# Two levels of Strassen for three quarters of a gated feed-forward network, with the weights' sums kept in DRAM

## The chip, the cores and the metric

The kernel runs on one core of a Trainium2 chip. The metric is the time of one execution on the device in microseconds. All data are float32.

## The reference

x has 32 rows of 64 tokens with 1024 features. Four layers are added to it, one after the other; ids choose the weights of each row:

```python
x = x + conv(x) * mask                       # a kernel K of 1024 steps, by FFT
x = x + einsum('bsi,boi->bso', x, w1[ids1])  # an adapter of 1024 x 1024 for each row
x = x + einsum('bij,bkj->bik', x, w2[ids2])  # another
gate = lora(x @ W_gate.T, A_gate, B_gate)    # W_gate, W_up: 2752 x 1024
up   = lora(x @ W_up.T, A_up, B_up)          # lora: a term of rank 16, by row
act  = silu(gate) * up
x = x + lora(act @ W_down.T, A_down, B_down) # W_down: 1024 x 2752
```

## The kernel before

Features lie on the partitions and tokens along the free axis. x is cut into four chunks of 512 tokens (eight rows). The convolution runs first, for all chunks. Then come the two adapters of the eight rows of chunk 0, and then, chunk by chunk, the feed-forward part `ffn`. While `ffn` works on a chunk, the 16 adapters of the next are slipped in between its pieces: `between` (L549) is called after every gate or up matrix of a tile and `other` (L543) after most pieces of W_down, and `other` emits an adapter when the shares handed to it say that one is due. In the first five calls `between` instead brings in the next chunk's x and adds the convolution to it (`bring`, `take`).

The 2752 hidden features are two halves of ten tiles of 128, and 192 that are left over (`rest`, L479). `gated` (L423) makes two tiles, m and m + 10, at a time, first gate, then up, each as a 2 x 2 block product in Strassen's form (Winograd's variant): `stationary` (L404) makes four sums of the four weight quarters on VectorE, and seven products replace eight. A product is four matmuls of 128 x 128 by 256 columns (L438), and each matmul is two instructions in the trace[...]. The order of the seven products, of the copies out of PSUM and of the adds is written out: 0, 5, 6, 4, 1, 2, 3. Product 4 overwrites the bank of product 5 and so needs that bank's reading done:

```python
            product(pa, 0, True)
            nc.scalar.copy(u, pa)
            product(pb, 5, True)
            nc.scalar.copy(cq[:, 3], pb)
            nc.vector.tensor_add(u, cq[:, 3], u)
            product(pc, 6, True)
            nc.vector.tensor_add(cq[:, 3], pc, u)
            product(pb, 4, True)
```

The rank-16 term of a tile is spread out by `expand` (L374) into four banks and copied by ScalarE into the tile `lt`, of which there is one; the add at L467 ends its use. After both matrices ScalarE takes the sigmoid, and VectorE multiplies twice.

W_down runs in two blocks of five m (`BLOCKS`), each after its gated tiles, by one level of Strassen as well (L630). Its moving sums come from act (`actd`, L587), its weights' sums from `stationary`, in segments of three m; the results are added into x. The rank term's columns of A_down are loaded by `columns` (L313), through the tile raw and eight DMAs of GpSimd's queue, and low_rank_down (L363) uses them after the first segment. `prepare` (L516) makes the four moving sums of x for the next chunk and copies three of its quarters on ScalarE (`xd`).

TensorE's order is the order of the program. The order of the other engines is set by a scheduler within what the dependences allow; within an engine instructions then start in that order. Weights come through `wpool`, nine buffers of 4 KB per partition in rotation, loaded by SP's queue. PSUM is eight banks in rotation (`ps_tile`). The pools apool, gpool and hpool hold what lives longer; a tile with `bufs=1` waits for the last use of the tile before it with the same tag.

Of the kernel before, what the change touches and what calls it, by code (L numbers as in the profile page):

```python
# [16 lines left out]
P = 128  # L17
# [10 lines left out]
BLOCKS = ((0, FM // 2), (FM // 2, FM))  # L28
MB = FM // 2
# [4 lines left out]
SEG = 3  # L34
TH = TC // 2
KH = KT // 2
R = 16
# [3 lines left out]
STEPS = 5  # L41
AT_GATED, AT_DOWN = 4, 5
# [27 lines left out]
def kernel(  # L70
# [18 lines left out]
    bd: bass.AP,  # L89
    wr: bass.AP,  # L90
# [212 lines left out]
    def b_rows(c, piece):  # L303
# [5 lines left out]
        tc.tile_pool(name="apool", bufs=MB, side="right", reuse_waits="tile")  # L309
    )  # L310
    cols = []

    def columns(table, c, n, name):  # L313

        raw = gpool.tile([P, BC, n, R], F32, tag="raw", name=f"raw_{name}", bufs=1)
# [47 lines left out]
    def low_rank_down(at, acts, name, last):  # L363
        v = gpool.tile([P, 2 * H], F32, tag="tv", name=f"tv_{name}", bufs=2)
        ps = low_rank(at, len(acts), lambda i: acts[i], name)
        nc.vector.tensor_mul(v, ps, bmask)
        if last is not None:
            nc.vector.tensor_add(v, v, last)
            for j in range(BC // 2):
                t = rest2[pair(j % 2), j // 2, 2 * H * (j % 2) :][:, : 2 * H]  # L370
                nc.vector.tensor_copy(t, v[pair(j)])
        return v
# [31 lines left out]
    def stationary(w, n, name):  # L404


        s = gpool.tile([P, 3, KH, P], F32, tag="s", name=f"s_{name}")
        a11, a12, a21, a22 = (w[i][:, k, :n, :] for i in (0, 1) for k in (0, 1))
        s1, s2, s4 = (s[:, i, :n, :] for i in range(3))
        nc.vector.tensor_add(s1, a21, a22)  # L410
        nc.vector.tensor_sub(s2, s1, a11)
        nc.vector.tensor_sub(a21, a11, a21)
        nc.vector.tensor_sub(s4, a12, s2)
        return a11, a12, s4, a22, s1, s2, a21
# [8 lines left out]
    def gated(c, m, xb, between):  # L423

        lt = expand(b_rows(c, m), f"{c}_{m}", (("g", 0), ("g", 1), ("u", 2), ("u", 3)))
        lt = lt.rearrange("p (g i) t -> p g i t", g=2)
        cs = []
        for g, w in enumerate((wg, wu)):
            name = f"{c}_{m}_{g}"
            wt = []  # L430
            for i in (0, 1):
                t = wpool.tile([P, 2, KH, P], F32, tag="w", name=f"wf{i}_{name}")
                nc.sync.dma_start(t.rearrange("p k s f -> p (k s f)"), w[i, m])
                wt.append(t)
            ws = stationary(wt, KH, name)
# [12 lines left out]
            pa, pb, pc = (ps_tile(f"pf{i}_{name}")[:, :TH] for i in range(3))  # L448
            cq = gpool.tile([P, 4, TH], F32, tag=f"c{g}", name=f"c_{name}", bufs=1)
            u = gpool.tile([P, TH], F32, tag="u", name=f"u_{name}")  # L450
# [3 lines left out]
            nc.scalar.copy(cq[:, 3], pb)  # L454
            nc.vector.tensor_add(u, cq[:, 3], u)
            product(pc, 6, True)
            nc.vector.tensor_add(cq[:, 3], pc, u)
            product(pb, 4, True)
            nc.vector.tensor_add(cq[:, 3], pb, cq[:, 3])  # L459
            product(pa, 1, False)  # L460
            nc.scalar.copy(cq[:, 0], pa)
            product(pb, 2, False)
            nc.vector.tensor_add(cq[:, 1], pb, u)  # L463
            product(pc, 3, False)
            nc.vector.tensor_add(cq[:, 2], pc, u)  # L465
            cf = cq.rearrange("p q t -> p (q t)")
            done = nc.vector.tensor_add(cf, cf, lt[:, g].rearrange("p i t -> p (i t)"))  # L467
            last_add.append(done.ins)
            cs.append(cq)
            between(2 * m + g)  # L470

        act = apool.tile([P, 2, TC], F32, tag="act", name=f"act_{c}_{m}")
        a = act.rearrange("p i (t n) -> p (i t) n", t=2)
        nc.scalar.activation(a, cs[0], AF.Sigmoid)
        nc.vector.tensor_mul(a, a, cs[0])
        nc.vector.tensor_mul(a, a, cs[1])
        return act

    def rest(c):  # L479


        bt = b_rows(c, FM)
        for i in range(3):
# [9 lines left out]
            elif i == 0:  # L493
                pss = []
                cr = gpool.tile([P, 3, KH, P], F32, tag="s", name=f"cr_{c}")
# [19 lines left out]

    def prepare(c, name):  # L516

        x_c = xs[c]
        at = columns(ag if name == "g" else au, c, KT, f"{name}_{c}")
# [10 lines left out]
        xd = hpool.tile([P, 7, KH, TH], F32, tag="xd", name=f"xd_{c}")  # L530
        for i, q in enumerate((0, 2, 3)):
            nc.scalar.copy(xd[:, 4 + i], xq[q])
        xb = moving(*xq, *(xd[:, i] for i in range(4)))
        return (xd[:, 4], xd[:, 5], xd[:, 6], *xb[3:])

    def ffn(c, xb, others):
# [6 lines left out]
        def other(share, of=(2 * FM - STEPS) * AT_GATED + (2 * KH - 3) * AT_DOWN):  # L543
# [4 lines left out]

        def between(i):  # L549

            if i < STEPS:
                if c + 1 < NCK:
                    if i in (2, 4):
                        take(c + 1, (i - 2, i - 1))
                    if i in (0, 2):
                        bring(c + 1, (i, i + 1))
            else:
                other(AT_GATED)

        rest(c)  # L560
        tv = None
        for block, (m0, m1) in enumerate(BLOCKS):
            last = m1 == FM
            n = 2 * MB + (0 if last else 2)
            at = columns(ad[:, block, :, :n], c, n, f"d{block}_{c}")
            acts = []
            for m in range(m0, m1):
                acts.append(gated(c, m, xb, between))
            ins = [act[:, i, :] for i in (0, 1) for act in acts]
            if last:  # L570


                wl = gpool.tile([P, 2, 2, L // 2], F32, tag="wl", name=f"wl_{c}", bufs=1)
# [6 lines left out]
            else:  # L580
# [3 lines left out]
            for i, act in enumerate(acts):  # L584
                t3 = apool.tile([P, 4, TH], F32, tag="actd", name=f"actd_{c}_{m0 + i}")
                q = [act[:, h, t * TH : (t + 1) * TH] for h in (0, 1) for t in (0, 1)]
                ab.append(moving(*q, *(t3[:, j] for j in range(4))))  # L587

            for h in range(KH):
# [9 lines left out]
                for s0 in range(m0, m1, SEG):  # L599
                    nt = min(SEG, m1 - s0)  # L600
                    end = s0 + nt == m1

                    more = int(end and not last)
                    at_ = s0 + block
# [12 lines left out]
                    elif end:  # L617
                        w = [[wl[:, t, i, h * P : (h + 1) * P] for i in (0, 1)] for t in (0, 1)]
                        tails = {1: (w[0][0], 0), 3: (w[0][1], 0), 4: (w[1][1], 1), 2: (w[1][0], 1)}
                    ws = stationary(wt, nt, f"{name}_{s0}")  # L620
                    for j in (0, 5, 6, 4, 1, 3, 2):
                        if end and j in tails:
                            w, t = tails[j]
                            a = rest2[:, t] if last else rest1[:, t * TH : (t + 1) * TH]
                            nc.tensor.matmul(  # L625
                                pss[j], w, a, start=False, stop=False, skip_group_check=True
                            )
                        for i in range(nt):
                            m = s0 + i
                            nc.tensor.matmul(  # L630
                                pss[j],
                                ws[j][:, i, :],
                                ab[m - m0][j],
                                start=(m == m0 and home[j] % 2 == 0),
                                stop=(m == m1 - 1),
                                skip_group_check=True,
                            )
                    if h == 0 and s0 == m0:
                        tv = low_rank_down(at, ins, f"d{block}_{c}", tv if last else None)
                u = gpool.tile([P, 3, TH], F32, tag="uo", name=f"uo_{name}", bufs=1)  # L640
# [21 lines left out]
                if not last or h < KH - 3:  # L662
# [319 lines left out]
def _layouts(np, v):  # L982
# [43 lines left out]


# [4 lines left out]
    wd = np.concatenate([wd[..., :MB, :], left1, wd[..., MB:, :]], axis=4)  # L1032
# [9 lines left out]
    a = a.reshape(2, 2, MB, P, NE, R).transpose(4, 1, 3, 0, 2, 5)  # L1042
# [71 lines left out]
```

## Time and profile before

| | us |
|---|---|
| median of three runs | 2381.4 (2378.52 to 2382.32) |
| the profiled execution: its own time | 2377.0 |
| its span | 2375.4 |
| convolution and first loads (0 to 191.9) | 191.9, TensorE busy 156.7, DMA share 0.93 |
| adapters of chunk 0 (191.9 to 343.88) | 152.0, TensorE busy 130.3, DMA share 1.01 |
| feed-forward part of chunk 2 | 536.9, TensorE busy 536.0, DMA share 0.62 |

The other three feed-forward parts are shown with the prediction. VectorE is busy for 256 us of the 537 us of a chunk, ScalarE for 66, GpSimd for 31. The matmuls in the records overlap (a row gives 381 ns for one whose successor starts 216 ns later), so a busy time is read as covered time and not as a sum of durations. Of the 505.41 MB that DMA moves, 15 MB are written to DRAM.

### The profile page before, as it was taken

How to read it: one execution, taken by the hardware profiler on the slowest of the kernel's cores; microseconds unless marked ns; L12 is line 12 of the kernel's file. 1: busy time of each engine (PE TensorE's matmuls, PEld its weight loads, DVE VectorE, ACT ScalarE, POOL GpSimd, SP SyncE). 2: the span in 40 equal slices, each digit the busy share in tenths (PEclk: the TensorE clock that was granted, in tenths of full speed). 3: DMA queues.
4: the chain of work that ended last, by engine and by line, in shares of the span. 5: the costliest groups of instructions: out<-in, count | busy, mean ns of one | idle time of the engine just before them, and what ended most of it. 6: DMA issues, size and time to landing. Idle time of an engine off the chain costs nothing.

```text
span 2375.4 us, 46146 instructions
## 1 busy us (share of the span) xinstructions
PE 2311.7 (97%) x19154; PEld 1839.0 (77%) x19154; DVE 1098.0 (46%) x2078; ACT 309.6 (13%) x605; POOL 190.3 (8%) x275
## 2 busy tenths in 40 slices
PE   5999889999999999999999999999999999999999
PEld 5986437777777787777777787777777787888888
DVE  7411116543355535543345535553445535554653
ACT  4200002100011102110011102110011102110210
POOL 4322001000000010000000010000000010000000
PEclk9999999999999999999999999999999999999999
DMA  8999994666766654666766654566766653223311
GB/s 300 368 342 361 407 391 125 217 229 218 268 228 246 210 164 139 206 239 218 278 219 243 219 169 132 202 245 222 271 222 233 223 163 112 80 78 109 96 56 63
DMA packets 165987, 505.41 MB, mean 213 GB/s; under 512 B 20354, under 2 KB 54402, under 8 KB 165266
## 3 DMA queue, kind: packets, MB, share of 16 engines
q1 hardware_dynamic: 147874, 463.87, 55.5%
q0 software_dynamic: 11104, 29.93, 3.7%
q10 hardware_dynamic: 6800, 8.65, 1.0%
q8 instruction: 151, 2.47, 0.4%
q14 instruction: 58, 0.48, 0.1%
HBM read 487.41 MB, written 14.97 MB: 211 GB/s over the span
## 4 chain that ended last, share of the span: by engine, by line
PE 90%; DMA 7%; DVE 2%; issue 1%; ACT 0%; SPq 0%; POOL 0%; DVEq 0%; ACTq 0%
PE pf L438 40%; PE po L630 21%; PE pa L269 16%; PE pc L915 4%; DMA wa<-in_w 4%; PE pr L499 4%; PE po L625 2%; PE pe L382 2%; DMA hk<-kp 1%; PE pl_d L354 1%; DVE x L232 0%; DMA wf<-in_wg 0%; DVE br L717 0%; PE pl_u L354 0%; PE pl_g L354 0%
## 5 line engine op out<-in xcount | busy, mean ns | idle before, releaser
L438 PE MATMUL pf<-xd,wf 128*128 128x256 f32 x2560 | 606.4, 381 | 0.0
L438 PEld LDWEIGHTS pf<-xd,wf 128*128 128x128 f32 x2560 | 481.9, 190 | 74.3 <-issue 6.2
L269 PE MATMUL pa<-wa,x 128*32 128x256 f32 x7872 | 453.4, 380 | 19.2 <-DMA wa<-in_w 17.1
L438 PE MATMUL pf<-xd,s 128*128 128x256 f32 x1920 | 454.1, 379 | 2.7 <-DVE c L459 2.2
L269 PEld LDWEIGHTS pa<-wa,x 128*32 128x32 f32 x7872 | 245.4, 110 | 216.0 <-DMA wa<-in_w 46.3
L438 PEld LDWEIGHTS pf<-xd,s 128*128 128x128 f32 x1920 | 364.3, 190 | 54.2 <-DVE c L459 3.7
L915 PE MATMUL pc<-uf,hk 128*128 128x256 f32 (+7 forms) x1024 | 151.7, 309 | 11.3 <-DMA hk<-kp 6.5
L630 PE MATMUL po<-act,wd 128*128 128x256 f32 x640 | 161.7, 383 | 0.0
L630 PE MATMUL po<-actd,s 128*128 128x256 f32 x640 | 159.0, 379 | 0.0
L630 PE MATMUL po<-actd,wd 128*128 128x256 f32 x640 | 159.0, 379 | 0.0
L915 PEld LDWEIGHTS pc<-uf,hk 128*128 128x128 f32 x1024 | 146.7, 193 | 15.6 <-issue 7.9
L296 POOL DMA_INDIRECT bgu<-in_bgu,rows x44 | 46.4, 1054 | 1328.7 <-PE pe L382 1257.8
L463 DVE TENSOR_TENSOR c<-pf,u 128x256 f32<-128x256 f32 x80 | 34.0, 425 | 235.3 <-PE pf L438 235.3
L630 PEld LDWEIGHTS po<-act,wd 128*128 128x128 f32 x640 | 119.5, 190 | 22.9 <-issue 6.3
L630 PEld LDWEIGHTS po<-actd,s 128*128 128x128 f32 x640 | 121.6, 190 | 16.5
L630 PEld LDWEIGHTS po<-actd,wd 128*128 128x128 f32 x640 | 121.6, 190 | 16.5
L392 ACT COPY lt<-pe 128x512 f32<-128x512 f32 x160 | 82.1, 599 | 335.8 <-PE pe L382 249.8
L279 DVE STREAM_TRANSPOSE y<-pa 128x512 f32<-128x512 f32 x64 | 45.6, 712 | 118.9 <-PE pa L269 118.9
L467 DVE TENSOR_TENSOR c<-c,lt 128x1024 f32<-128x1024 f32 x80 | 98.0, 1224 | 5.5 <-DVE c L465 0.5
L410 DVE TENSOR_TENSOR s<-wf 128x512 f32<-128x512 f32 x80 | 54.9, 686 | 87.9 <-DMA wf<-in_wg 45.5
L410 DVE TENSOR_TENSOR s<-wd 128x384 f32<-128x384 f32 x64 | 31.2, 488 | 133.8 <-PE po L630 87.4
L499 PE MATMUL pr<-x,wr 128*128 128x512 f32 x192 | 84.2, 595 | 0.0
(169 smaller groups left out, 1830.8 us busy)
## 6 DMA issues: line engine op xcount, KB each, us to landing
wa<-in_w SPq DMA_DIRECT2D x492, 512.0 KB, 7.5
wf<-in_wg SPq DMA_DIRECT2D x80, 512.0 KB, 3.9
wf<-in_wu SPq DMA_DIRECT2D x80, 512.0 KB, 3.7
wd<-in_wd SPq DMA_DIRECT2D x96, 384.0 KB, 4.6
hk<-kp SPq DMA_DIRECT2D x30, 1024.0 KB, 8.4
x<-in_xt SPq DMA_DIRECT2D x4, 2048.0 KB, 11.1
uf<-in_xf SPq DMA_DIRECT2D x16, 512.0 KB, 5.3
early<-in_w SPq DMA_DIRECT2D x16, 512.0 KB, 6.3
```

The source lines that it names most:

```text
L269: nc.tensor.matmul(acc[i * S : (i + 1) * S, s * 256 : (s + 1) * 256], xs[c][:, kt, lo + s * S : lo + (s + 1) * S], wt[:, i * 256 : (i + 1) ...
L279: nc.vector.transpose(y, acc)
L296: nc.gpsimd.indirect_dma_start(out=t, out_offset=None, in_=table, in_offset=bass.IndirectOffsetOnAxis(ap=at_, axis=0),)
L382: nc.tensor.matmul(ps[:, at_ * 2 * H : (at_ + 1) * 2 * H], bt[pair(j), g], tms[table][pair(j)], start=(g == 0), stop=True, skip_group_chec ...
L392: nc.scalar.copy(lt[:, :n, 2 * H * j : 2 * H * (j + 1)], ps[:, : n * 2 * H].rearrange("p (i t) -> p i t", i=n),)
L410: nc.vector.tensor_add(s1, a21, a22)
L438: nc.tensor.matmul(ps, ws[j][:, kt, :], xb[j][:, kt, :], start=start and kt == 0, stop=kt == KH - 1, skip_group_check=True,)
L467: done = nc.vector.tensor_add(cf, cf, lt[:, g].rearrange("p i t -> p (i t)"))
L499: nc.tensor.matmul(ps, wt[:, kt, :], xs[c][:, kt, :], start=(kt == 0), stop=(kt == KT - 1),)
L625: nc.tensor.matmul(pss[j], w, a, start=False, stop=False, skip_group_check=True)
L630: nc.tensor.matmul(pss[j], ws[j][:, i, :], ab[m - m0][j], start=(m == m0 and home[j] % 2 == 0), stop=(m == m1 - 1), skip_group_check=True,)
L915: nc.tensor.matmul(ps[:, j, d * B :], hk[:, j, d * P : (d + 1) * P], uf[:, i + j, : KT - d, :].rearrange("p k b -> p (k b)"), start=(d == ...
```

## The change

W_gate and W_up of chunks 1 to 3 are multiplied by two levels of Strassen. `gated` now handles two m at once (a group gi, five in a chunk): it runs one pass for gate and one for up, in chunk 0 by `halves`, afterwards by `quarters`.

- `halves` keeps the matmuls of before for the two m. Beside them VectorE makes the second level's sums of the weights (`kept`, four times in a pass), and GpSimd's queue writes these and the first level's sums (`kept_parts`) to tiles in DRAM (`sums`, `parts`).
- `quarters` runs seven outer products (the second index of `xb`), each made of seven inner ones of two matmuls with 128 columns. The outer products go in units: three pairs, (0, 5), (1, 6) and (4, 2), and a single one, (3,). A pair shares its PSUM banks and its tile `t`, of which there is one. Weights and their sums are loaded from a new input `wq`, `parts` and `sums`, two tiles (`wb`, `wa`) to an outer product. Three banks serve a pair, four the single unit.
- The sigmoid, the multiply by it and the second multiply are done in two halves of 1024 columns.
- `prepare` makes 7 x 7 tiles of moving sums for chunks 1 to 3.
- W_down has three blocks, of two, four and four m. A_down's columns are requested after a block's gated tiles and share the tag of `t`, as does the tile `uo` of W_down's evictions; `wl` has the tag of `lt`, and the columns of A_gate and A_up that of the sigmoid's tile.
- The shares by which adapters are slipped in are new, and `between` is called after the second pair and at the end of a pass.

```diff
-BLOCKS = ((0, FM // 2), (FM // 2, FM))
-MB = FM // 2
+BLOCKS = ((0, 2), (2, 6), (6, FM))
+MB = 4
+MG = 2
+NG = FM // MG
...
-SEG = 3
+SEG = (2, 4, 2)
...
-AT_GATED, AT_DOWN = 4, 5
+AT_GATED, AT_DOWN = 3, 5
...
+        raw = gpool.tile([P, BC, n, R], F32, tag=tag, name=f"raw_{name}", bufs=1)
...
+    def sides(a11, a12, a21, a22, s1, s2, s3, s4):
+        nc.vector.tensor_add(s1, a21, a22)
+        nc.vector.tensor_sub(s2, s1, a11)
+        nc.vector.tensor_sub(s3, a11, a21)
+        nc.vector.tensor_sub(s4, a12, s2)
+        return a11, a12, s4, a22, s1, s2, s3
...
+    def low_rank_of(c, gi, g):
+        name = f"{c}_{gi}_{g}"
+        lt = expand(b_rows(c, 2 * gi + g), name, [("gu"[g], i) for i in range(4)])
+        return lt.rearrange("p (i m) t -> p i m t", i=2)
...
+    def halves(c, gi, g, o, xb, between):
+        name = f"{c}_{gi}_{g}"
+        w = (wg, wu)[g]
+        lt = low_rank_of(c, gi, g)
+        wts, sts, sides_of = [], [], []
...
+            st = s_tile((gpool, qpool[0])[m], f"{name}_{m}")
+            wts.append(wt)
+            sts.append(st)
+            sides_of.append(stationary(wt, KH, st))
...
+        def kept(q):
+            src = [
+                [wts[m][0] for m in range(MG)],
+                [wts[m][1] for m in range(MG)],
+                [sts[m][:, 0:2] for m in range(MG)],
+                [sts[m][:, 2:3] for m in range(MG)],
+            ][q]
+            n = 1 if q == 3 else 2
+            t = qpool[0].tile([P, 2, 4, KQ, P], F32, tag="kept", name=f"kept{q}_{name}", bufs=2)
+            a11, a12, a21, a22 = (
+                src[m][:, :, k * KQ : (k + 1) * KQ, :] for m in range(MG) for k in range(2)
+            )
+            sides(a11, a12, a21, a22, *(t[:, :n, i] for i in range(4)))
+            nc.gpsimd.dma_start(
+                sums[2 * gi + g][2 * q : 2 * q + n].rearrange("j p e -> p j e"),
+                t[:, :n].rearrange("p j i k f -> p j (i k f)"),
+            )
...
+            if m == 0:
+                kept_parts()
+            kept(2 * m)
...
+            kept(2 * m + 1)
+            o_m = o[:, :, m]
+            done = nc.vector.tensor_add(o_m, o_m, lt[:, :, m])
+            between()
+        last_add.append(done.ins)
...
+    def quarters(c, gi, g, o, xb, between):
+        name = f"{c}_{gi}_{g}"
+        lt = low_rank_of(c, gi, g)
+        at_sums = {0: 0, 1: 1, 6: 2, 3: 3, 4: 4, 5: 5, 2: 6}
+        at_parts = {6: 0, 4: 1, 5: 2, 2: 3}
+        raw = {0: 0, 1: 1, 3: 2}
+        def load(j):
+            tb = wpool.tile([P, 3, KQ, P], F32, tag="w", name=f"wb{j}_{name}")
+            src = wq[2 * gi + g, raw[j]] if j in raw else parts[2 * gi + g][at_parts[j]]
+            nc.sync.dma_start(tb.rearrange("p i k f -> p (i k f)"), src)
+            ta = wpool.tile([P, 4, KQ, P], F32, tag="w", name=f"wa{j}_{name}")
+            nc.sync.dma_start(
+                ta.rearrange("p i k f -> p (i k f)"), sums[2 * gi + g][at_sums[j]]
+            )
...
+        def unit(js):
+            n = len(js)
+            ws = [load(j) for j in js]
+            def product(ps, i, start):
+                for w, j, to in zip(ws, js, range(n)):
+                    for k in range(KQ):
+                        nc.tensor.matmul(
+                            ps[:, to * TQ : (to + 1) * TQ],
+                            w[i][:, k, :],
+                            xb[:, j, SLOT[i], k, :],
+                            start=start and k == 0 and to == 0,
+                            stop=k == KQ - 1,
+                            skip_group_check=True,
+                        )
+            js_ = "".join(map(str, js))
+            banks = [ps_tile(f"pq{i}_{name}_{js_}")[:, : n * TQ] for i in range(5 - n)]
+            pa, pb, pc, pd = (banks + banks[1:2])[:4]
+            t = gpool.tile([P, 4, 2 * TQ], F32, tag="t", name=f"t_{name}_{js_}", bufs=1)
+            c11, c12, c21, c22 = (t[:, i, : n * TQ] for i in range(4))
+            u = gpool.tile([P, 2 * TQ], F32, tag="u", name=f"u_{name}_{js_}")[:, : n * TQ]
+            product(pa, 0, True)
+            nc.scalar.copy(u, pa)
+            product(pb, 5, True)
+            nc.scalar.copy(c22, pb)
+            nc.vector.tensor_add(u, c22, u)
+            product(pc, 6, True)
+            nc.vector.tensor_add(c22, pc, u)
+            product(pd, 4, True)
+            nc.vector.tensor_add(c22, pd, c22)
+            product(pa, 1, False)
+            nc.scalar.copy(c11, pa)
+            for i in (3, 2) if n == 1 else (2, 3):
+                ps, to = ((pd, c12), (pc, c21))[i - 2]
+                product(ps, i, False)
+                nc.vector.tensor_add(to, ps, u)
...
+        add = nc.vector.tensor_add
+        c11, c12, c21, c22 = quarter(o)
+        l11, l12, _, _ = quarter(lt)
+        p1, p6 = unit((0, 5))
+        add(c12, p1, p6)
+        add(c11, p1, l11)
+        p2, p7 = unit((1, 6))
+        add(c21, c12, p7)
+        add(c11, c11, p2)
+        between()
+        p5, p3 = unit((4, 2))
+        add(c22, c21, p5)
+        add(c12, c12, p5)
+        add(c12, c12, p3)
+        (p4,) = unit((3,))
+        add(c12, c12, l12)
+        add(c21, c21, p4)
+        done = add(o[:, 1], o[:, 1], lt[:, 1])
+        last_add.append(done.ins)
+        between()
+    def gated(c, gi, xb, between):
+        f = quarters if c else halves
+        act = apool.tile([P, 2, MG, TC], F32, tag="act", name=f"act_{c}_{gi}")
+        f(c, gi, 0, act, xb, lambda: between(2 * gi))
+        sg = gpool.tile([P, 2, MG, TC], F32, tag="cu", name=f"sg_{c}_{gi}", bufs=1)
+        for i in (0, 1):
+            nc.scalar.activation(sg[:, i], act[:, i], AF.Sigmoid)
+            nc.vector.tensor_mul(act[:, i], act[:, i], sg[:, i])
+        up = gpool.tile([P, 2, MG, TC], F32, tag="cu", name=f"up_{c}_{gi}", bufs=1)
+        f(c, gi, 1, up, xb, lambda: between(2 * gi + 1))
+        for i in (0, 1):
+            nc.vector.tensor_mul(act[:, i], act[:, i], up[:, i])
         return act
...
+        for i in (0, 1):
+            b11, b12, b21, b22 = (q_of(k, t)[i] for k in (0, 1) for t in (0, 1))
+            moving(b11, b12, b21, b22, *(at_(j)[i] for j in (4, 5, 6, 3)))
+            for j, q in zip(range(3), (b11, b21, b22)):
+                nc.scalar.copy(at_(j)[i], q)
+        b11, b12, b21, b22, t1, t2, t4 = (xd[:, :, i] for i in range(7))
+        moving(b11, b12, b21, b22, t1, t2, b12, t4)
...
-        def other(share, of=(2 * FM - STEPS) * AT_GATED + (2 * KH - 3) * AT_DOWN):
+        def other(share, of=4 * (NG - 1) * AT_GATED + (KH + 1) * AT_DOWN):
...
+            if i >= 2:
                 other(AT_GATED)
+            elif c + 1 < NCK:
+                came_at[0] += 1
+                if came_at[0] == 1:
+                    bring(c + 1, (0, 1))
+                if came_at[0] == 3:
+                    take(c + 1, (0, 1))
+                    bring(c + 1, (2, 3))
...
-            at = columns(ad[:, block, :, :n], c, n, f"d{block}_{c}")
+            n = 2 * (m1 - m0) + (0 if block else 2)
             acts = []
-            for m in range(m0, m1):
-                acts.append(gated(c, m, xb, between))
-            ins = [act[:, i, :] for i in (0, 1) for act in acts]
+            for gi in range(m0 // MG, m1 // MG):
+                acts.append(gated(c, gi, xb, between))
+            at = columns(ad[:, block, :, :n], c, n, f"d{block}_{c}", "t")
...
-                wl = gpool.tile([P, 2, 2, L // 2], F32, tag="wl", name=f"wl_{c}", bufs=1)
+                wl = gpool.tile([P, 2, 2, L // 2], F32, tag="lt", name=f"wl_{c}", bufs=1)
...
-                u = gpool.tile([P, 3, TH], F32, tag="uo", name=f"uo_{name}", bufs=1)
+                        tv = low_rank_down(at, ins, f"d{block}_{c}", tv, last)
+                u = gpool.tile([P, 3, TH], F32, tag="t", name=f"uo_{name}", bufs=1)
...
+                if block == 0 and h == 1 and c + 1 < NCK:
+                    take(c + 1, (2, 3))
+                if block == 1 or (last and h < KH - 3):
...
```

## The prediction

> **What bounds the kernel now.** First the page's busy shares and the row of the granted clock, then the windows by chunk, then the chain of waits, then the matmul groups split by shape, last the timeline of one gated layer.
>
> ```profile
> PE 2311.7 (97%) x19154; PEld 1839.0 (77%) x19154; DVE 1098.0 (46%) x2078; ACT 309.6 (13%) x605; POOL 190.3 (8%) x275
> ...
> PEclk9999999999999999999999999999999999999999
> ```
>
> TensorE is busy throughout at full clock. The windows cut the span at the starts of the four chunks' feed-forward parts (columns: TensorE, its weight loads, VectorE, ScalarE, GpSimd, clock, DMA share, GB/s):
>
> ```profile
> 343.88:881.17 537.29, 536.14 (x4497) 422.30 (x4498) 255.61 (x474) 68.84 (x134) 36.87 (x58) 1.00 0.61 214
> 881.17:1417.61 536.44, 535.83 (x4498) 422.12 (x4497) 256.02 (x474) 66.10 (x132) 31.11 (x46) 1.00 0.62 214
> 1954.48:2375.40 420.92, 416.79 (x2320) 354.55 (x2319) 218.94 (x433) 58.57 (x126) 11.59 (x11) 1.00 0.28 86
> ```
>
> A chunk with adapters to slip in takes 537 us, the last 421, with no gap on TensorE. The chain of waits prices its pieces:
>
> ```profile
> 274.88 10.11 DMA wa<-in_w
> ...
> 443.49 7.04 PE pa L269 x128
> ...
> 2027.33 1.10 PE pe L382 x32
> 2028.43 24.37 PE pf L438 x112
> 2052.80 1.10 PE pe L382 x32
> ```
>
> Each row of reduced tiles (m) costs 24.37 + 1.10 = 25.47 us, back to back; an adapter 7.04 us. Before the feed-forward part an adapter's eight 512 KB loads take 10.2 us from start to start (274.88 to 285.10): 4.19 MB / 10.2 = 410 GB/s is what DMA can give.
>
> ```profile
> L438 PE MATMUL pf<-xd,wf 128*128 128x256 f32 x2560 | 606.4, 381 | 0.0
> ...
> L915 PE MATMUL pc<-uf,hk 128*128 128x160 f32 x128 | 28.1, 302 | 0.0
> ...
> L915 PE MATMUL pc<-uf,hk 128*128 128x128 f32 x128 | 24.8, 276 | 0.0
> L915 PE MATMUL pc<-uf,hk 128*128 128x96 f32 x128 | 23.3, 264 | 0.0
> ```
>
> The new matmuls have 128 columns, a form the convolution has. Its matmuls come in pairs of equal shape whose busy times overlap: a pair covers the step plus one duration, so the step is 24.8/64 us - 276 ns = 111 ns for 128 columns, 137 for 160, 100 for 96[...]. A 256-column one takes 24.37 us / 112 = 217.6 ns. Half the columns cost half the time, just.
>
> ```profile
> 2027.91 0.42 DVE L465 TENSOR_TENSOR c<-pf,u 128x256 f32<-128x256 f32 x1
> 2028.84 1.23 DVE L467 TENSOR_TENSOR c<-c,lt 128x1024 f32<-128x1024 f32 x1
> 2030.10 1.22 DVE L476 TENSOR_TENSOR act<-act,c 128x1024 f32<-128x1024 f32 x1
> 2030.16 2.05 ACT L392 COPY lt<-pe 128x512 f32<-128x512 f32 x4 [5.87 <-DVE c L467]
> 2032.04 0.42 DVE L418 TENSOR_TENSOR actd<-act,actd 128x256 f32<-128x256 f32 x1
> 2032.07 0.42 ACT L452 COPY u<-pf 128x256 f32<-128x256 f32 x1
> 2032.34 0.43 ACT L454 COPY c<-pf 128x256 f32<-128x256 f32 x1
> 2032.49 0.43 DVE L420 TENSOR_TENSOR actd<-act,actd 128x256 f32<-128x256 f32 x1
> 2033.65 1.89 PE L438 MATMUL pf<-xd,s 128*128 128x256 f32 x8
> ```
>
> This is the start of an m. The four copies of the low-rank term wait for the last add of the m before; the copies out of PSUM queue behind them and end at 2032.77; the fourth product, which overwrites that bank, starts at 2033.65. So the cover is 0.9 us, with products of 1.73 us (8 x 216 ns).
>
> [...] In the timeline the next add starts 0.34 us after a 256 one, 0.45 if it needs its result; for 512: 0.61 and 0.72, for 1024: about 1.15 and 1.26. [...]
>
> **The change part by part.** A pass is gate or up for two m's: ten in a chunk.
>
> Matmuls. A pass was 2 x 112/2 matmuls, 24.37 us; in chunks 1 to 3 it is 7 x 7 x 2 matmuls of two instructions: 196 x 0.111 = 21.76. Saved 2.6 us, x30 = **-78 us**. W_down, tails, rank terms, adapters keep their matmuls.
>
> The single unit. The seven outer products run as three pairs and a single one. A pair's product lasts 8 x 0.111 = 0.89 us, the single one's 0.44. Let E be the end of the third pair on TensorE. VectorE then owes, in the changed program's order, before the single unit's first add: c21 (starts E+0.2), three 512 adds out of t at 0.65, 1.26, 1.87 and the add of l12 at 2.59; the single's adds start at 3.2, 3.5, 3.8. Its sixth product accumulates onto the bank that the second of these reads: due at 5 x 0.44 = 2.2, it starts at 3.9. **1.7 us** lost, all 30 times; in the up passes a 1024 multiply stands in between: **2.85**. TensorE has nothing else in its order there.
>
> Into the next pass. After gate: a sigmoid multiply (1.15) sits between the single's adds, so the last add on act ends at 8.1; ScalarE does the second sigmoid (1.06, to 9.2), only then four low-rank copies (2.05), then the two PSUM copies, to 11.9. The next pass's fourth product is due at 3.1 + 1.1 + 2.7 = 6.9. It starts at 12.0: 5.1 us lost, the 1.7 included. After up, with lt free at 8.4: 2.85 + 1.5 + 0.4 = 4.75. If an adapter (7.04) lies between, it hides all but 2.1 and 3.2.
>
> Into W_down. Blocks 0 and 1 now start on the m's just made. Product two needs half 1 of act and its moving sums (start about 12 instead of 6.8): 8.3 lost before block 0; before block 1 7.3, or 3.0 with an adapter. raw for A_down shares t's slot and is requested after the block's passes: slot free at 7.8, eight GpSimd issues 7.4 us (1383.06 to 1390.43 in the trace), landing 2.8, copy 1.1: 19. Before block 2 TensorE wants it at 12.0: 2.85 + 7 = 9.9.
>
> Sums. Chunk 3 has no adapters: five 5.1, two 4.75, 8.3, 7.3, 9.9 = 60.5. In chunks 1 and 2 the shares of other() put an adapter at five of the eight pass ends of groups 1 to 4: 5.1 + 8.3 + 2.1 + 3.2 + 5.1 + 3.0 + 5.1 + 3.2 + 2.1 + 9.9 = 47. Together **+155 us** (bounds 95 and 180: the adds may close up[...]).
>
> Chunk 0. The same matmuls. VectorE gets, per pass, three times four 512 adds and four 256 ones: 3 x 4 x 0.65 + 4 x 0.37 = 9.3 us on 13.6 (4 x 0.65 x 2 sums of weights, 6.0 evictions, 2.4 multiplies), beside 25.5 of TensorE: fits on average, but the sums of the next pass's weights stand behind the last pass's multiplies, and 12 us of sums ahead of its first evictions. I work out 7.6 us for a pass without an adapter ahead and 2 with one; the first group is ordered better, and W_down's stages hide some. Four of the first and four of the second: 38; **+40** (10 to 90, as waits for kept buffers can't be seen here). Writes of 5.2 MB a pass, 52 MB in all, go beside the loads.
>
> DMA in chunks 1 and 2. A pass loads 7 x (393 + 524 KB) = 6.4 MB, and 1.3 adapters 5.5 MB: 11.9 MB in 21.8 + 1.1 + 9.3 = 32 us, 370 GB/s of 410. Nine buffers, four in use by a pair, hold one pair ahead; after an adapter in mid-pass the next pair's tiles come some 2 us late, five times a chunk: **+20** for both (0 to 80).
>
> Rest. The next chunk's xd sums, 14 us of VectorE instead of 5, spread over W_down's 14 us steps; a third block's evictions, with uo and t in one slot, delay the next pass by about 1 us: **+8** (0 to 20).
>
> Sum: -78 + 155 + 40 + 20 + 8 = +145. On the profiled execution's 2377.0 us: 2522; its time lies 4 us under the median of the runs, so **2525 us** is forecast.
>
> **The rivals.**
> - Faster (0.10). TensorE runs ahead: eight banks hold two pairs, and the adds that I put in the way are off its path. Then 78 us stay, less 20 in chunk 0: 2320. For it: VectorE is 46% busy. Against: the single unit's last two products reuse banks of the same unit. It decides if a pass loses under 2.6 us on average and chunk 0 nothing; I have 5.
> - DMA bound (0.12). If 3 KB rows and mixed writes give 300 GB/s, the eight passes with adapters last 95.4 MB / 300 = 318 us a chunk, not 260: +115 less the hidden +20: 2620.
> - Chunk 0 bound by VectorE and by kept buffers waiting for their writes (0.15): +100 in place of 40: 2585.
> - The waits are half as long (0.08): -78 + 78 + 50 = 2425.
> - No change (0.02): losses equal the gain.
>
> **How the numbers follow.** My own case has 0.53; the bounds of its terms, not all at one end at once, give 2405 to 2630, which also takes in the second, third and fourth rivals and leaves out the first. A difference under 0.2% can't be told from none here. Faster 0.10, same 0.02, slower 0.88.
>
> **What would show it.** 128-column steps of 111 ns in pq[...]. Per pass without adapters a gap on TensorE near 1.7 us in the single unit, ended by VectorE, and one near 3.4 us at the fourth product of the next pass, ended by ScalarE. Last part: about 455 us instead of 421. Chunk 0: 575 or more. Waits of pq for wa or wb above 40 us would be the DMA rival. I am wrong if TensorE stays gapless, or if the last chunk gets shorter.

## The result, and the profile after

The changed kernel takes 2628.2 us (median of four runs, 2623.9 to 2643.5), the one before 2380.7 on the same chip: a ratio of 1.105, with a 95% interval of 1.100 to 1.110. The forecast was 2525, slower by 6.0%, with a range up to 2630. The direction holds, the loss is 1.7 times the forecast one, and the measured time lies at the very end of the range, by the ratio (1.105 x 2380.7 = 2631) just beyond it. The profiled execution took 2624.3 us, with a span of 2622.6.

The page of the changed kernel, its busy shares and the row of the granted clock:

```profile
PE 2349.9 (90%) x21674; PEld 1918.9 (73%) x21674; DVE 1356.9 (52%) x2746; ACT 369.9 (14%) x814; POOL 267.2 (10%) x387
...
PEclk9999999999999998999999999999999999999999
```

TensorE's share fell from 97% to 90%. The row of tenths hides what the mean clock says: 0.967, against 1.0 before. The windows, cut at the starts of the chunks' feed-forward parts (columns as in the prediction; the clock is the third number from the end):

```profile
342.90:946.35 603.45, 561.20 (x4500) 431.81 (x4497) 359.53 (x687) 68.53 (x141) 91.51 (x126) 0.97 0.76 275
946.35:1549.12 602.77, 541.92 (x5337) 446.80 (x5336) 309.47 (x628) 85.81 (x200) 35.53 (x54) 0.96 0.74 262
1549.12:2146.00 596.88, 536.36 (x5338) 439.50 (x5337) 308.98 (x628) 85.54 (x200) 34.76 (x54) 0.97 0.74 265
2146.00:2622.60 476.60, 423.67 (x3161) 382.66 (x3159) 266.96 (x579) 80.07 (x192) 24.72 (x36) 0.94 0.51 171
```

The four parts are 66, 66, 60 and 56 us longer than before. TensorE is idle for 42 to 61 us in each (length less busy time), where it was 1 to 4. And it is busier than before, though chunks 1 to 3 have 26 us less of matmul work each. The clock tells much of why: a value of 0.94 over 476.6 us means some 57 us at half clock in the last part. In the clock's record there are 37 such stretches, each at 0.5, nearly all of 3.4 or 6.8 us, 171 us in all; TensorE was busy in 149 of them, and half of that is 74 us.

The waits of TensorE in the last part, where there are no adapters (columns: who waits, for what, us in total, times, longest):

```profile
PE pq L574 <- DVE t L595: 26.5, 10, 5.1
PE pq L574 <- ACT t L592: 10.5, 6, 2.6
PE po L835 <- DVE actd L438: 5.7, 3, 3.0
PE pl_d L368 <- ACT at_d L345: 4.7, 1, 4.7
PE pq L574 <- DVE t L597: 1.6, 1, 1.6
```

The first row is the single unit's sixth product behind VectorE, the second the next pass's fourth product behind ScalarE, then the entries into W_down and A_down's columns. These are the waits that the prediction named; only the last row, 1.6 us, is another. The timeline from a gate pass to the next up pass shows both, and what follows a wait:

```profile
2288.47 0.69 DVE L628 TENSOR_TENSOR act<-act,t 128x512 f32<-128x512 f32 x1
2289.08 0.68 DVE L629 TENSOR_TENSOR act<-act,t 128x512 f32<-128x512 f32 x1
2289.80 0.69 DVE L630 TENSOR_TENSOR act<-act,t 128x512 f32<-128x512 f32 x1
2290.52 0.69 DVE L632 TENSOR_TENSOR act<-act,lt 128x512 f32<-128x512 f32 x1
...
2291.52 0.29 DVE L595 TENSOR_TENSOR t<-pq,u 128x128 f32<-128x128 f32 x1
2291.87 0.71 PE L574 MATMUL pq<-xd,wb 128*128 128x128 f32 x4 [1.73 <-DVE t L595]
...
2292.96 1.89 PE L397 MATMUL pe<-tm_u,bgu 32*128 32x128 f32 x32
...
2294.77 2.04 PE L574 MATMUL pq<-xd,wb 128*128 128x128 f32 x8
2296.64 1.95 PE L574 MATMUL pq<-xd,wa 128*128 128x128 f32 x16
2296.94 2.02 ACT L407 COPY lt<-pe 128x512 f32<-128x512 f32 x4
...
2299.10 0.42 ACT L592 COPY t<-pq 128x256 f32<-128x256 f32 x1
...
2299.57 1.16 PE L574 MATMUL pq<-xd,wa 128*128 128x128 f32 x8 [0.98 <-ACT t L592]
```

Four adds of the old units stand ahead of the single unit's (L595), and TensorE waits 1.73 us. Then its work runs at half speed (granted clock 0.50 in the window 2293.23:2296.64): the rank matmuls take 1.89 us (1.10 in the kernel before) and the product of eight 2.04, where the 16 matmuls of the next row take 1.95. The wait behind ScalarE is then only 0.98 us; where the clock had stayed up ahead of it, it was 2.57. So slow matmuls partly fill the next wait, and their cost can't simply be added to it.

### The profile page after: what moved, and what is told of

The parts are those of the page before. It is cut to its first block, busy times and chain, and to the rows that moved or that the text cites. A ratio compares the mean times of both kernels' runs of the same rounds, so it can differ in the third digit from the quotient of the medians.

```text
span 2622.6 us, 53347 instructions
## 1 busy us (share of the span) xinstructions
PE 2349.9 (90%) x21674; PEld 1918.9 (73%) x21674; DVE 1356.9 (52%) x2746; ACT 369.9 (14%) x814; POOL 267.2 (10%) x387
## 4 chain that ended last, share of the span: by engine, by line
issue 55%; PE 18%; DMA 4%; DVE 4%; POOL 2%; POOLq 1%; ACT 0%; DVEq 0%; ACTq 0%
PE po L835 9%; PE pf L506 5%; PE pa L273 2%; POOL bgu L300 1%; DMA wa<-in_w 1%; POOLq L334 1%; DMA wf<-in_wu 1%; DMA wd<-in_wd 1%; DMA wf<-in_wg 1%; DMA raw_d<-in_ad 1%; POOL raw_d L340 1%; DMA sums<-kept 0%; PE pl_d L368 0%; DVE s L421 0%; DVE s L423 0%
## 5 line engine op out<-in xcount | busy, mean ns | idle before, releaser
L574 PE MATMUL pq<-xd,wa 128*128 128x128 f32 x3360 | 437.6, 281 | 35.7 <-ACT t L592 25.9
L574 PEld LDWEIGHTS pq<-xd,wa 128*128 128x128 f32 x3360 | 409.4, 196 | 43.2 <-ACT t L592 29.4
L574 PE MATMUL pq<-xd,wb 128*128 128x128 f32 x2520 | 350.0, 285 | 96.9 <-DVE t L595 75.1
L574 PEld LDWEIGHTS pq<-xd,wb 128*128 128x128 f32 x2520 | 315.5, 197 | 114.7 <-DVE t L595 80.8
L603 DVE TENSOR_TENSOR t<-pq,u 128x256 f32<-128x256 f32 x240 | 92.4, 390 | 169.1 <-PE pq L574 168.9
L506 PE MATMUL pf<-xd,wf 128*128 128x256 f32 x640 | 159.1, 394 | 0.0
L506 PE MATMUL pf<-xd,s 128*128 128x256 f32 x480 | 124.1, 405 | 29.2 <-DVE act L529 17.5
L506 PEld LDWEIGHTS pf<-xd,wf 128*128 128x128 f32 x640 | 126.2, 199 | 22.7 <-issue 2.9
L506 PEld LDWEIGHTS pf<-xd,s 128*128 128x128 f32 x480 | 94.7, 200 | 48.9 <-DVE act L529 20.3
L593 DVE TENSOR_TENSOR u<-t,u 128x256 f32<-128x256 f32 x120 | 46.8, 390 | 126.0 <-ACT t L592 126.0
```

The source lines that it names most:

```text
L506: nc.tensor.matmul(ps, ws[j][:, kt, :], xb[j][:, kt, :], start=start and kt == 0, stop=kt == KH - 1, skip_group_check=True,)
L574: nc.tensor.matmul(ps[:, to * TQ : (to + 1) * TQ], w[i][:, k, :], xb[:, j, SLOT[i], k, :], start=start and k == 0 and to == 0, stop=k == K ...
L593: nc.vector.tensor_add(u, c22, u)
L603: nc.vector.tensor_add(to, ps, u)
```

## The experiments

All kernels are read part by part (chunk by chunk) beside the changed kernel and each other. E1 to e9 have one execution each. Parts with the same work differ between executions: chunk 0 took 596.8 to 605.4 us in four with the changed kernel's code there, chunk 2 596.9 to 604.7, the last part 471.3 to 476.6. Smaller differences decide nothing. E1, e2, e4, e5, e7 and e8 ask which part of the change costs what; e3, e6 and the last pair ask about the clock; e9 and e10 try to mend it.

**Without the kept sums.** `kept` and `kept_parts` aren't called, and the loads of `quarters` are

```diff
-            src = wq[2 * gi + g, raw[j]] if j in raw else parts[2 * gi + g][at_parts[j]]
+            src = wq[2 * gi + g, j % 3]
...
-                ta.rearrange("p i k f -> p (i k f)"), sums[2 * gi + g][at_sums[j]]
+                ta.rearrange("p i k f -> p (i k f)"), (wg, wu)[g][j % 2, MG * gi]
```

> Chunk 0 doesn't make or write the second level's sums; chunks 1 to 3 load tiles of the same sizes from the input tensors instead, so their weights are not the right ones. My theory (the kept sums hold VectorE, which waits for their writes, and TensorE waits for VectorE): chunk 0's part goes from 603 to 540-548 us, the other parts stay within 5 us, 2565 us in all (2555 to 2578). Rival (the grouping of two m, the third block and the shared tiles cost it): chunk 0 stays above 590.

2582.4 us. Chunk 0 took 562.8: 41 us less than with the sums, but 26 more than before, so neither my theory nor the rival was right alone.

**One level everywhere.** `gated` always takes `halves`, without kept sums.

> All chunks run the one-level passes of chunk 0, without kept sums: what remains of the change is grouping, three blocks of W_down, shared tiles. My theory (the second level's waits and the half clock after them make the loss): parts of 540 to 548 us and 425 to 430 for the last, 2405 us in all (2390 to 2425), hardly any half-clock time. Rival (grouping and blocks): above 2480.

2478.4 us; the windows of chunks 1 and 3:

```profile
914.00:1475.10 561.10, 542.87 (x4498) 423.30 (x4497) 268.25 (x521) 67.06 (x137) 36.40 (x54) 0.99 0.60 204
...
2034.50:2476.70 442.20, 424.68 (x2321) 356.38 (x2319) 231.99 (x479) 61.30 (x132) 25.07 (x35) 0.99 0.29 86
```

My expectation here forgot what the prediction itself had priced, the entries into W_down: TensorE waits 9.1 us at W_down's matmuls in chunk 3. The parts are 21 to 27 us longer than before, 95 us in all, without any second level. From this kernel to the changed one the kept sums add 39 us in chunk 0, and the second level 42, 38 and 34 us in chunks 1 to 3, where it should have saved 26 each.

**Matmuls in the waits.** `fill` issues n matmuls into a PSUM bank that nobody reads:

```diff
+            if c == 3 and js == (0, 5) and (g, gi) != (0, 0) and not (g == 0 and gi in (1, 3)):
+                fill(c, name + "a", 5 if g else 2)
             product(pd, 4, True)
...
+            if n == 1:
+                fill(c, name + "b", 5 if g else 3)
             for i in (3, 2) if n == 1 else (2, 3):
```

> The changed kernel with 256-column matmuls that nobody reads put where TensorE waits: in every single unit before its sixth product (3 of them after gate, 5 after up), and in chunk 3 before the fourth product of a pass's first pair too. They take 0.435 us each, less than the wait. My theory (the waits set the clock to half for 3.4 us or more each): although TensorE has 30 us more to do in chunk 3, its part goes from 477 to 455-465 us, its half-clock time from 56 us to under 25, its idle time from 53 to 15-25; chunks 1 and 2 get 5 to 12 us shorter each; 2590 us in all. Rival (the half clock comes from the 128-column form and its many weight loads): half-clock time stays above 45 us in chunk 3, no part gets shorter, 2620 to 2640.

2619.2 us. Half-clock time fell from 171 us to 102, in chunk 3 from 56 to 15, and chunk 3 took 467.8 us with 30 us more work (471.3 to 476.6 in four executions without it). So the half clock depends on the waits, with the form of the matmuls unchanged; but the gain was smaller than I expected. The pair at the end puts a number on it.

**Adds written later, low-rank copies behind the PSUM copies.** `t` and the tiles that share its tag have two buffers, and `middle` emits the adds of the unit before (for the first pair: `low_rank_of`):

```diff
             nc.vector.tensor_add(c22, pd, c22)
+            middle()
             product(pa, 1, False)
```

> t and its tag have two buffers; the adds of a unit's results are written behind the fourth product of the next unit; the low-rank term is spread out after the fourth product of the first pair, so its four copies stand behind the two PSUM copies on ScalarE. My theory (the queue order on VectorE and ScalarE makes the waits): the single unit's wait falls from 1.73 and 2.67 us to about 1 (some old adds still stand between), the wait at the next pass's fourth product to under 1; chunk 3 from 477 to 435-448, chunks 1 and 2 from 600 to 565-580, 2530 us in all (2500 to 2560). Rival (TensorE waits for loads or for VectorE's total work): no part gets more than 10 us shorter.

2560.4 us. In chunk 3 the waits for VectorE within a pass fell from 28.1 us to 9.4, and those for ScalarE were gone:

```profile
PE pq L572 <- DVE t L593: 8.8, 10, 2.4
PE pl_d L368 <- ACT at_d L345: 5.8, 1, 5.8
PE po L846 <- DVE actd L438: 4.1, 3, 2.5
PE po L846 <- DVE act L661: 1.9, 1, 1.9
```

Chunk 3 took 435.3 us, 41 less, as expected: the order on the two queues made these waits. It is now below the 442.2 of e2, the one-level kernel with the same three blocks, but above the 421.0 of the kernel before: only beside the first does the second level pay there. Chunks 1 and 2 took 588 and 592, only 15 and 5 less: 16 us of waits for `wb` and `wa` stay in chunk 1, and the entry waits too.

**Sums made, but not written.** As e1, with the sums of `kept` kept and both writes taken out.

> Chunk 0 makes the kept sums but doesn't write them or the parts to DRAM; chunks 1 to 3 load tiles of the same sizes from the input tensors, so their weights are not the right ones. Chunk 0's part was 603 us with sums and writes and 563 with neither. My theory (VectorE stands still at a kept tile whose write hasn't landed): 566 to 578. Rival (the sums themselves are too much for VectorE): 590 or more.

2610.0 us, chunk 0 at 585.7: above my range and below the rival's. The sums on VectorE cost 23 us (585.7 - 562.8), their writes 18 (603.5 - 585.7), a figure not far above the spread of that part. Without the writes TensorE's waits for VectorE in the gated products hardly change (24.0 us with, 21.9 without); its waits for adapters' loads, 5.0 us, are gone, and the half clock is 24 us instead of 41.

**Waits of set length in the kernel before.**

```diff
             product(pb, 5, True)
+            if g == 1:
+                for _ in range((0, 8, 10, 13)[c]):
+                    nc.scalar.copy(cq[:, 3], u)
             nc.scalar.copy(cq[:, 3], pb)
```

> The kernel before with extra copies on ScalarE ahead of the copy that the fourth product of each up matrix waits for: none in chunk 0, 8, 10 and 13 in chunks 1, 2 and 3, for ten waits a chunk of about 1.0, 1.9 and 3.2 us. My theory (a wait of about 2 us or more is followed by 3.4 us at half clock): chunk 0 stays at 537; chunk 1 gets 10-14 us longer, with few half-clock windows; chunk 2 22-32 with some 5 windows; chunk 3 45-55, of which 32 are idle and the rest ten windows. Rival (a wait costs its own length): 10, 19 and 32 us and no half clock.

2491.3 us; chunks 1 to 3, and the matmuls behind one wait of 3.9 us:

```profile
885.85:1439.49 553.64, 539.85 (x4497) 422.55 (x4496) 256.65 (x474) 98.34 (x212) 31.40 (x46) 1.00 0.61 207
1439.49:2006.68 567.19, 544.75 (x4498) 426.09 (x4496) 256.55 (x474) 106.35 (x232) 31.58 (x46) 0.99 0.59 202
2006.68:2489.50 482.82, 439.78 (x2321) 368.00 (x2319) 219.97 (x433) 109.94 (x256) 11.58 (x11) 0.95 0.26 76
```

```profile
2051.21 2.51 PE L438 MATMUL pf<-xd,s 128*128 128x256 f32 x8 [3.90 <-ACT c L457]
2053.51 3.11 PE L438 MATMUL pf<-xd,wf 128*128 128x256 f32 x8
2056.46 1.89 PE L438 MATMUL pf<-xd,s 128*128 128x256 f32 x8
```

Products of 1.89 us take 2.51 and 3.11 after the wait. Chunk 3 got 61.9 us longer (421.0 before) for 39.0 us of idle time: each wait of 3.9 us cost 6.2. Sorted by length: of five waits of 0.9 us none was followed by half clock, of ten between 1.7 and 1.9 one, of five between 2.6 and 2.8 four, of ten of 3.9 all. Here a wait cost more than its length once half clock followed it, and the longer waits were followed by it more often; where they fell is counted in the last section.

**Two blocks of W_down in the one-level kernel**: blocks (0, 4) and (4, 10), in segments of 2 and 3. Some adapters of the next chunk run ahead of the second half of its convolution's adds here; their number and size is the same.

> The one-level kernel (e2) with two blocks of W_down, of four and six m, in place of three. My theory (each entry into a W_down block that starts on the m just made costs 5 us or more of waiting, and half clock after it): the parts go from 561 to 552-557, the last from 442 to 434-438, 2450 us in all. Rival (the passes of two m cost it, through ScalarE's copies of the low-rank term): parts within 3 us of the one-level kernel's.

2428.0 us. The parts took 550.6, 553.7, 553.3 and 426.2, so 6 to 16 us less. In chunk 3 the 9.1 us of waits at W_down's matmuls are gone, and the 10 us of half clock too; with whatever else the third block and the other segments cost, that is three quarters of the one-level kernel's loss there. In chunks 1 and 2 waits for adapters' weights grew (5.9 us in chunk 1).

**Everything deferred.** As e4, with the single unit's adds first and the gating written into the next pass; the third pair's adds are put behind with

```diff
+        with tc.issue_after(adds[-1]):
+            add(c22, c21, p5)
+            add(c12, c12, p5)
+            add(c12, c12, p3)
+            add(c12, c12, l12)
```

> As the later adds (e4), and: the third pair's adds and the low-rank add stand behind the single unit's own adds on VectorE; the sigmoid and the multiplies of a pass are written into the next pass, behind its fourth product; A_down's columns are requested after a block's first gate pass, through the tile of actd. My theory: in chunk 3 the single unit's wait falls below 0.5 us, no wait for ScalarE is left, the wait for A_down's columns is gone: 435 to 412-424. Chunks 1 and 2 keep their waits for DMA (16 to 20 us): 590 to 565-580. Chunk 0 595-605. 2510 us in all (2485 to 2535). Rival (VectorE's work as a whole is too much): waits for VectorE above 15 us stay in chunk 3.

2564.8 us, chunk 3 at 445.0: a miss, 10 us worse than e4 (chunks 1 and 2 took 584 and 588, 4 less each). TensorE's waits in chunk 3:

```profile
PE pq L578 <- DVE t L601: 9.2, 8, 1.8
PE po L886 <- issue: 6.9, 1, 6.9
PE po L886 <- DVE act L684: 5.9, 1, 5.9
PE po L886 <- DVE rest L389: 5.9, 1, 5.9
```

The waits within the passes (pq) did not fall, 12.5 us in all and 9.4 in e4. Those at W_down's matmuls (the three rows of po) grew from 6.7 to 18.7 us, more than the 5.8 us of waiting for A_down's columns that went away. That they wait for the deferred work, which has to be done there at once, is likely but not shown: one row names no releaser.

**Entries.** As e4, with A_down's columns requested after a block's first gate pass and an adapter at each entry of blocks 2 and 3.

> The later adds (e4), with A_down's columns requested after a block's first gate pass, through the tile of actd, and with one adapter moved to each entry of the second and third block of W_down (chunks 0 to 2). My theory (the entries into W_down wait for the m just made and for the columns): the wait of the rank matmuls for the columns (5.8 us in chunk 3, 8.7 in chunk 1) is gone, chunk 3 goes from 435 to 427-432, chunks 1 and 2 from 590 to 570-582, their waits for loads (16 us) stay; 2530 us in all (2510 to 2548). Rival (another wait takes the place of each): parts within 4 us of e4's.

2583.6 us. The wait for the columns is gone, but in chunk 1 the matmuls of W_down now wait 10.6 us for its weights' sums (7.0 in e4), which stand behind other work on VectorE. Chunks 1 to 3 took 594.9, 597.0 and 438.4 us, so none got shorter than in e4, as the rival said: other waits took the place of this one.

**Kept sums placed by hand.** As e9, with

```diff
+            with tc.issue_after(done.ins):
+                kept(2 * m)
```

behind the third add of an m, and the same behind its last.

> As e9, and in chunk 0 the kept sums of VectorE are put behind the add that frees the fourth product's bank (two of the four) or behind the last add of an m (the other two), where TensorE has 3.4 us to run. My theory (in chunk 0 TensorE waits because kept sums stand ahead of the evictions, sums and writes about half each): chunk 0 from 597 to 568-582, its waits for VectorE from 26 us to under 8; the other parts as in e9; 2510 us in all (2488 to 2532). Rival (VectorE's total work, or the kept tiles' writes alone): chunk 0 stays above 588. Either way it stays above the kernel before.

2564.2 us, 1.078 times the time before (1.076 to 1.079). Chunk 0 took 592.6 us, 15 less than e9's but only 4 less than the shortest of the four with the changed kernel's code there. My theory had 568 to 582, and the rival 588 or more; the whole was expected at 2510. Its waits:

```profile
PE pa L273 <- DMA wa<-in_w: 15.5, 15, 2.5
PE po L861 <- DVE wd L425: 5.8, 1, 5.8
PE po L861 <- issue: 5.3, 1, 5.3
PE pf L509 <- DVE act L532: 3.8, 2, 2.2
```

The gated products' waits for VectorE fell from e9's 23.7 us to 5.2, as my theory said; but TensorE then waits 15.5 us for the adapters' loads, where it was 7.9 in e9 (and 0.3 in e1, without sums and writes). So 7.6 of the 18.5 us went into the next limit.

**The clock, timed.** The changed kernel and the kernel of e3, four runs each on one chip.

> The changed kernel again, beside e14 on the same chip: 2620 to 2645 us, with half-clock time of 140 to 190 us in the profiled execution. It is the base for e14.

> The kernel of e3 (matmuls that nobody reads in the waits of the single units, and in chunk 3 at the fourth product too), timed. If half-clock time costs its full half, the 50 to 80 us of it that e3 had less save 25 to 40 us: 2590 to 2603. If much of it runs where the next wait would be anyway, as in chunk 3 of e3, the saving is under 15 us: 2613 to 2630. I expect the second.

2629.9 us (ratio to before 1.103, 1.099 to 1.106) and 2608.1 us (1.095, 1.093 to 1.097). I expected under 15 us of gain and it was 22. In the profiled executions half-clock time fell from 174 to 92 us. In chunks 1 to 3, where the filling is, it fell by 72 us, and these parts were 22.7 us shorter together: about a third of a microsecond for each, not a half. (The mean clocks of all runs, 0.967 and 0.9795, give the same third.) Two things lower it, and these runs don't separate them: some slow matmuls only fill a wait that comes anyway, and the filling is itself 65 us of work that may outlast a wait. If a third holds for all 171 us, the half clock costs the changed kernel some 54 us; that is worked out, not measured.

## Why the prediction fell short

What held:
- The matmuls. Eight of the 128-column form take 0.89 us, 111 ns for each step, as forecast.
- The single unit: 1.73 us after gate and 2.67 after up, forecast 1.7 and 2.85. The next pass's fourth product waits 2.57 us at full clock, forecast 3.4.
- The entries in chunk 3: 7.2, 7.9 and 7.8 us, forecast 8.3, 7.3 and 9.9.
- The sign, and the sum of the idle time: it rose by 60, 60 and 49 us in chunks 1, 2 and 3, where the waits and loads of the prediction come to 57, 57 and 61. The sum is close partly by luck. In chunk 3 the waits behind ScalarE are 10.5 us instead of 21: after the two up passes there is none, and after two gate passes it is 0.98 us, in all four where the clock had been halved just ahead.

What failed is the sum of the waits: "+155" and the "+40" of chunk 0 priced a wait at its own length. The step that is missing is the matmuls after it. In chunks 1 to 3 the forecast had a loss of 103 us (145 less the 42 of chunk 0), and it was 182. Idle time rose by 169 us, where 181 were forecast; but TensorE's busy time, which was to fall by 78, rose by 13. Of these 91 us the half clock makes 55, half of the 111 us in which TensorE was busy at it there. Beside the one-level kernel the same shows: the prediction's own terms for the second level in chunk 3 come to 9 us (35 of waits within the passes less 26 of matmuls), and e2 gives 34.

The trace of the kernel before has a clock of 1.000 and no half clock to price, and the forecast has no term for it. In the changed kernel's trace 27 of the 37 stretches last 3.413 us, the others two to four times as long, and waits shorter than that suffice: in e6 four of five between 2.6 and 2.8 us. With gross 74 us, of which some 54 count by the estimate above, this is the largest term that was left out.

The other terms, measured against the forecast:
- Chunk 0 lost 66 us instead of 42 (40 and its quarter of the rest). What was left out is 27 us from grouping, the three blocks and shared tiles, which e2 loses there without any kept sum: the prediction priced the entries into W_down for chunks 1 to 3 alone. The kept sums cost some 39 us, forecast 38, but partly by luck: all of it was put on VectorE's sums, and the writes were to go beside the loads, while e5 has about 23 for the sums and 18 for the writes. The rival of the kept buffers saw something real, since VectorE stands still for the writes (5.47 us at 473.8 in the trace); but by e5 TensorE's waits for VectorE hardly depend on it.
- Waits for loads in chunks 1 and 2 were 15 us each, instead of 10.
- The other 36 of the 91 us of TensorE's busy time are neither more work nor half clock. In e6 each wait added 0.2 us beyond idle time and half clock; for the 86 waits of chunks 1 to 3 that makes about half of it (an estimate from e6), and the rest stays open.

The other rivals: "faster" falls, since the adds that stand in the way are on TensorE's path (e4 takes them away and gains 41 us in chunk 3). "Waits half as long" falls, since the idle time came to 169 of 181 us. DMA alone doesn't bind: it is 0.74 to 0.76 busy at 262 to 275 GB/s (the 300 GB/s of that rival was a supposition, not measured), and pq's waits for wb and wa are 14.9 and 12.5 us in chunks 1 and 2, under the 40 that were named as its sign. But these waits stay when those for VectorE go (16.3 us in e4's chunk 1). No kernel with the second level that was tried comes near the one before; the best are e4 (2560.4, one run) and e10 (2564.2).

## What to carry to other kernels

A change that takes TensorE from gapless to many waits of 2 or 3 us is to be priced at more than these waits: in e6 a wait of 3.9 us cost 6.2 us, and where waits were dense (e13 against e14) about a third of the half-clock time was left as cost. In no trace here did the half clock set in after a window of 3.4 us with less than 1.5 us of idle time in it, short waits added up: the last section has the count. The finer products gave VectorE and ScalarE less time to follow (a product lasts 0.89 us, 1.73 before), and the order in which they take evictions and old sums then counted: e4's order took the waits for VectorE within chunk 3's passes from 28.1 us to 9.4. The order has to be laid out with the split. And a saving of 26 us in a chunk is small against three entries of 8 us: count the places where a stage starts on what was just made before counting the matmuls saved.

## What was not expected of the hardware

- Waits of the same length may or may not be followed by half clock: one of ten of 1.7 to 1.9 us in e6, seven of 21 of 1.5 to 2 us in the changed kernel. What tells them apart in the traces is where they fall. All half-clock stretches of an execution begin on one grid of 3.413 us (the changed kernel's 37 within 5 ns), and each follows a grid window in which TensorE was idle for over 1.5 us. Counted over the 13 traces of changed kernels and experiments, from the first feed-forward part on: of 7530 windows at full clock with under 1.5 us of idle time none was followed by half clock, of 222 with over 2.0 us all were, and of 239 in between 70 (in the changed kernel's trace alone none of 556, all of 30, and seven of 30). Here are two waits of 1.73 us in the last part, each with its window and the next (columns as above):

```profile
2289.81:2293.23 3.42, 1.69 (x19) 1.37 (x22) 3.05 (x6) 1.49 (x3) 0.00 (x0) 1.00 0.87 322
2293.23:2296.64 3.41, 3.41 (x40) 3.19 (x37) 2.65 (x5) 0.66 (x1) 1.42 (x1) 0.50 0.78 281
...
2347.84:2351.25 3.41, 2.23 (x41) 1.99 (x41) 3.04 (x8) 1.41 (x3) 0.00 (x0) 1.00 0.78 241
2351.25:2354.67 3.42, 2.91 (x28) 2.72 (x24) 2.26 (x3) 1.53 (x3) 1.01 (x1) 1.00 0.84 326
```

  The first lies in one window, which leaves TensorE busy for 1.69 us, and half clock follows. The second is cut by the grid; 2.23 us are busy, and the clock stays. A wait of 3.9 us puts at least 1.95 us into one window wherever it falls, in line with ten of ten in e6.
- So the half-clock time differs from execution to execution: the last part, with the same work, took 471.3, 472.4, 474.0 and 476.6 us, with 27 to 56 us at half clock.
- The runs of the changed kernel spread from 2619 to 2644 us, 0.9%, those of the kernel before from 2378 to 2388, 0.4%.
